# Layer 0 of a four-layer graph network: division as the outputs leave PSUM, first and last norms in halves, and a new order of the matmuls

## The chip, the core and the metric

The kernel runs on one core of a Trainium2 chip, in one launch. The metric is the device time of that launch in microseconds (us). TensorE (PE) multiplies matrices into PSUM (eight banks of 128 x 512 fp32); VectorE (DVE) and ScalarE (ACT) work elementwise; GpSimd (POOL) does little here; SyncE (SP) issues the transfers.

## The reference, cut to what is computed

32 graphs of 512 nodes with 256 features pass through four layers. Each layer is followed by a residual and a norm over the 256 features.

```
x = ln(x + L0(x, adj))   # 4 heads of 64: edges with weights leaky_relu(s_i + d_j), softmax over the edges,
                         # relu(attention @ h + bias) + h, then a norm over each head's 64 columns
x = ln(x + L1(x, adj))   # one head of 256: softmax(relu(s_i + d_j)) over the edges, elu
x = ln(x + L2(x, adj))   # 8 heads of 32, scaled dot products, symmetric edges; norm, feed-forward 256-1024-256, norm
x = ln(x + L3(x, adj))   # one head of 256: softmax(leaky_relu(s_i + d_j)) over the edges
```

The adjacency holds 0 and 1 with ones on the diagonal, so of layer 0's five edge types one occurs. All matmuls but layer 2's scores are in fp32.

## The kernel before

Rows are 128 nodes: a graph is R = 4 rows, its features K = 2 column blocks. `fast_path` does the work; `general_path` is run only when a verdict, kept in `ok` and `sums`, says that the inputs lie outside what the fast path takes.

**The order of the work.** `graph(b)` (L802) is a generator that goes through the stages of graph b: edges, layer 0, layer 1, mask, qkv, attention, projection, feed forward, layer 3. At every `yield`, `paced` (L111) gives out a place, `PERIOD * b` plus an entry of the table `PLACES` (L28), and `heapq.merge` (L832) always continues the graph with the lowest place. With PERIOD 12054, stages of several graphs interleave: layer 0 of one graph runs beside layer 1 of the same, layer 2 of the one before, and layer 3 of another. `tc.manual_schedule` (L831) keeps PE's instructions in exactly that order. The other engines' queues are ordered by a scheduler; each of them works strictly in the order it was given. So the table decides where in PE's stream each group of matmuls stands, and indirectly the rest.

**Layer 0** (L411). For each of four rows, `h0p` gives h and the edge terms; ACT takes exponentials into `ex` and into the last column of `hv` (65 columns a head: 64 values and one weight); DVE adds the bias (L431) and multiplies the values by the weight (L436). Four transposes of a broadcast column (`along`, `gp`, copied by ACT into `gb`) lay out one term per head. Then four blocks j = 0 to 3, one for each row of source nodes. For each block DVE makes four tiles `pt`, one per head (`kept`, L404/L407, 128 x 512). PE then multiplies: for each head two products of 32 value columns with the head's `pt` into `o`, and one product into `den`, whose stationary operand is the head's last 32 columns of `hv`, the weight being the last of them. A product with 32 stationary columns writes 32 rows of PSUM: one of four column groups of the array. The two banks `ops` hold heads 0 and 1, and heads 2 and 3; a head's two halves lie in neighbouring groups:

```
for hh in range(H):
    for e in range(0, HO, DH):
        matmul(ops[hh // 2][hh % 2 * HO + e : hh % 2 * HO + e + DH, :], hv[:, j, hh, e : e + DH], pt[hh])
for hh in range(H):
    matmul(den[hh * DH : (hh + 1) * DH, :], hv[:, j, hh, HC - DH :], pt[hh])
```

So PE's stream in a block is o (head 0, two), o (head 1, two), o (head 2, two), o (head 3, two), den (four). After block 3, ACT copies den and the two o out (`back`, L464), PE transposes each in four pieces (`backp`), DVE takes the reciprocals of den's transposed columns into `rd` (L477), multiplies and applies relu out of PSUM (L484), adds h (L493), and goes on with the norm over heads (`head_layernorm`, L288: sums, differences, squares on ACT, variances, a root by Ln and Exp, a product), gamma (L495), x (L496) and the norm over features (`layernorm`, L268: statistics per row, Ln and Exp for the root, one ACT instruction L280 per row). The next step is layer 1's transposes `xt1p`.

The tiles `pt`, `gb`, `back`, `sq`, `squares`, `relu` and `exp` of stages "a" (layers 0 and 1, edges) share nine buffers (`part`, L257).

**Around layer 0 in PE's stream**, in a middle graph: f2p and f1p of the feed forward, three `o` groups of layer 1 (o<-h,pt, 128 columns), h0p, gp, s (scores), cp, xt3p, block 0, h3p, xt2p, gp, den of layer 2, block 1, qkp, wop (four rows; each row is added by DVE at L680, and the statistics follow), qkp, blocks 2 and 3, four `o` of layer 3 (evacuated by DVE at L752 and L753), ytp, backp, vp, then scores and feed forward.

**The end of a graph.** `feed_forward` (L683) adds the last f2p (L720), then a norm, gamma (L722), x (L723) and another norm for all four rows; layer 3 (L728) divides each row, norms all four, and one transfer of 512 KB writes them (L823).

Of the kernel before, what the change touches and what calls it, by code (L numbers as in the profile page):

```python
# [9 lines left out]
F32 = mybir.dt.float32  # L10
# [18 lines left out]
    "edges": [-3978, -1720, -957, -79],  # L29
    "x": [5375],  # L30
    "mask": [14366, 15324, 18155, 20933],
    "layer 0": [
        -33568, -33515, -33424, -32942, 5301, 7043, 7043, 7043, 8766, 10194, 11091, 11128,
        11993, 11993, 14391,
    ],
    "layer 1": [15460, 15460, 15555, 15555, 15555, 15555, 16382, 17321, 17344, 17344, 17355, 17355],
    "qkv": [18153, 18153, 22255, 22255, 23139, 24065, 25534, 25534, 25534, 25534, 25534],
    "attention": [
        -5960, -4506, -4506, -3927, 26460, 26497, 26497, 26593, 26886, 27435, 27446, 27462,
        28434, 28434, 28779, 29106, 29409, 30200, 31616, 32371, 34290, 34290,  # L40
    ],
    "projection": [34382, 34412, 34412, 34412, 34443],
    "feed forward": [
        36011, 36047, 37566, 38431, 38431, 38519, 38519, 38646, 38646, 38732, 38732, 39499,
        39499, 39646, 39646, 40873, 41200, 41449, 41464,
    ],
    "layer 3": [44919, 44919, 44969, 44969, 44969, 44969, 45682, 48065, 48065, 48065, 48422, 48422],
}
# [24 lines left out]
def fast_path(ctx: ExitStack, tc: tile.TileContext, a: dict, out: bass.AP, bad: bass.AP):  # L73
# [20 lines left out]
    HC = HO + 1  # L94
    ND = R * (H + 2)
    NL = 6
    NV = R * (NL + H) + 2 * K

# [161 lines left out]

    def all_rows(v):
        return v.unsqueeze(1).to_broadcast([P, R, D])

# [3 lines left out]

    def layernorm(y, e, mv):  # L268

        st = buf([P, R, 6], "bn", "bn", 2)  # L270
        rs = buf([P, 2, R], "rs", "rs", 2)
        for r in range(R):
            nc.vector.bn_stats(st[:, r, :], y[:, r, :])  # L273
            nc.vector.bn_aggr(mv[:, r, :], st[:, r, :])  # L274
        inverse_root(rs[:, 0, :], mv[:, :, 1], e)
        nc.vector.scalar_tensor_tensor(  # L276
            rs[:, 1, :], mv[:, :, 0], -1.0, rs[:, 0, :], op0=ALU.mult, op1=ALU.mult
        )
        for r in range(R):
            nc.scalar.activation(  # L280
                y[:, r, :],
                y[:, r, :],
                AF.Identity,
                bias=rs[:, 1, r : r + 1],
                scale=rs[:, 0, r : r + 1],
            )

    def head_layernorm(y, e, var):  # L288

        G = R * H  # L290
        yg = y.rearrange("p r (g d) -> p (r g) d", g=H)
        st = buf([P, 2, G], "lnh", "st", 2)
        nc.vector.tensor_reduce(st[:, 0, :], yg, axis=X, op=ALU.add)
        nc.vector.tensor_scalar_mul(st[:, 0, :], st[:, 0, :], 1.0 / HO)
        nc.vector.tensor_sub(yg, yg, st[:, 0, :].unsqueeze(2).to_broadcast([P, G, HO]))
        for i in range(2):
            g = slice(i * G // 2, (i + 1) * G // 2)
            sq = part("sq").rearrange("p (g d) -> p g d", d=HO)
            nc.scalar.activation(sq, yg[:, g, :], AF.Square, scale=HO**-0.5)
            nc.vector.tensor_reduce(var[:, g], sq, axis=X, op=ALU.add)  # L300
        inverse_root(st[:, 1, :], var, e)
        nc.vector.tensor_mul(yg, yg, st[:, 1, :].unsqueeze(2).to_broadcast([P, G, HO]))

# [106 lines left out]

    def layer0(x, xt, at, rd, mv, var):  # L411
        h = buf([P, R, D], "h", "h0", 2)
# [28 lines left out]
        for j in range(R):  # L441
            pt = [kept("pt0", gbs[hh], at[:, j, :], ex[:, 1, hh, j : j + 1]) for hh in range(H)]
            yield
            for hh in range(H):
                for e in range(0, HO, DH):
                    product(nc.tensor.matmul,
                        ops[hh // 2][hh % 2 * HO + e : hh % 2 * HO + e + DH, :],
                        hv[:, j, hh, e : e + DH],
                        pt[hh],
                        start=j == 0,  # L450
                        stop=j == R - 1,
                    )
            for hh in range(H):
                product(nc.tensor.matmul,
                    den[hh * DH : (hh + 1) * DH, :],
                    hv[:, j, hh, HC - DH :],
                    pt[hh],
                    start=j == 0,
                    stop=j == R - 1,
                )  # L460
        back = []
        for i, o in enumerate((den, *ops)):
            t = part("back")
            nc.scalar.copy(t, o)  # L464
            back.append(t)
        y = sb.tile([P, R, D], F32, tag="y", name="y0", bufs=3)
        for i in range(1 + H // 2):
            yield
            p = bank("backp")
            for r in range(R):  # L470
                product(nc.tensor.transpose,
                    p[:, r * P : (r + 1) * P], back[i][:, r * P : (r + 1) * P], ident
                )
            if i == 0:
                rdh = rd.rearrange("p (i r h) -> p i r h", i=H // 2, r=R)
                for i in range(H // 2):
                    nc.vector.reciprocal(  # L477
                        rdh[:, i],
                        p.rearrange("p (r h e) -> p r h e", r=R, h=H)[
                            :, :, 2 * i : 2 * i + 2, DH - 1  # L480
                        ],
                    )
                continue
            nc.vector.scalar_tensor_tensor(  # L484
                y[:, :, (i - 1) * P : i * P].rearrange("p r (h e) -> p r h e", h=2),
                p.rearrange("p (r h e) -> p r h e", r=R, h=2),
                0.0,
                rdh[:, i - 1].unsqueeze(3).to_broadcast([P, R, 2, HO]),
                op0=ALU.max,
                op1=ALU.mult,  # L490
            )
        nc.vector.tensor_add(x, x, all_rows(bet0))
        nc.vector.tensor_add(y, y, h)  # L493
        head_layernorm(y, 1e-6, var)
        nc.vector.tensor_mul(y, y, all_rows(gam0))  # L495
        nc.vector.tensor_add(y, y, x)  # L496
        layernorm(y, 1e-5, mv[0])
        return y

# [14 lines left out]

    def layer1(x, at, rd, mv):
        xt = yield from transposed([x[:, r, :] for r in range(R)], "xt1")
# [8 lines left out]
        for r in range(0, R, 2):  # L525
# [9 lines left out]
            nc.vector.scalar_tensor_tensor(xr, y, -1.0, xr, op0=ALU.add, op1=ALU.add)  # L535
        layernorm(x, 1e-5, mv[1])
        return x
# [144 lines left out]

    def feed_forward(x, y, mv):  # L683
        layernorm(y, 1e-5, mv[2])
        yt = yield from transposed([y[:, r, :] for r in range(R)], "yt")
# [4 lines left out]
        for r in range(0, R, 2):  # L690
# [29 lines left out]
            nc.vector.tensor_add(yr, acc, yr)  # L720
        layernorm(y, 1e-5, mv[3])
        nc.vector.tensor_mul(y, y, all_rows(ln2g))  # L722
        nc.vector.tensor_add(y, y, x)  # L723
        layernorm(y, 1e-5, mv[4])
        return y


    def layer3(x, at, rd, mv):  # L728
        xt = yield from transposed([x[:, r, :] for r in range(R)], "xt3")
# [20 lines left out]
        for r in range(R):  # L750
# [4 lines left out]
            )  # L755
        layernorm(x, 1e-5, mv[5])
        return x

    ends = [0, R * H, R * (H + 1), ND]
    def load_x(b):  # L760
# [8 lines left out]

    def layer0_all(b, x, xt, at, rd, mv, var):  # L770
        if b == 0:
            bcast(bet0, "bet0")
            bcast(gam0, "gam0")
        return (yield from layer0(x, xt, at, rd, mv, var))

    def layer1_all(b, x, at, rd, mv):
        if b == 0:
            weights13(w1g, "w1g", "a1")
        return (yield from layer1(x, at, rd, mv))

# [11 lines left out]
    def feed_forward_all(b, x, y, mv):  # L792
        if b == 0:
            weights_ff()
        return (yield from feed_forward(x, y, mv))

    def layer3_all(b, x, at, rd, mv):
        if b == 0:
            weights13(w3g, "w3gt", "a3")
        return (yield from layer3(x, at, rd, mv))  # L800

    def graph(b):  # L802
        yield PERIOD * b + PLACES["edges"][0]
        rd = sb.tile([P, ND], F32, tag="rd", name="rd", bufs=3)
        mvs = sb.tile([P, 2 * NL * R + H * R + 2 * K], F32, tag="mvs", name="mvs", bufs=3)
        mv = [mvs[:, 2 * i * R : 2 * (i + 1) * R].rearrange("p (r s) -> p r s", s=2) for i in range(NL)]
        tops = mvs[:, 2 * NL * R :]
        var, spread = tops[:, : H * R], tops[:, H * R :]
        rds = [rd[:, ends[i] : ends[i + 1]] for i in range(3)]
        if b == 0:  # L810
            xt, x = yield from paced(b, "x", load_x(b))
        at = yield from paced(b, "edges", mask(b))
        if b:
            xt, x = yield from paced(b, "x", load_x(b))
        x = yield from paced(b, "layer 0", layer0_all(b, x, xt, at, rds[0], mv, var))
        x = yield from paced(b, "layer 1", layer1_all(b, x, at, rds[1], mv))
        a2 = yield from paced(b, "mask", symmetric(b, at))
# [3 lines left out]
        x = yield from paced(b, "feed forward", feed_forward_all(b, x, y, mv))  # L821
        x = yield from paced(b, "layer 3", layer3_all(b, x, at, rds[2], mv))
        nc.sync.dma_start(out[b].rearrange("(r p) d -> p r d", p=P), x)  # L823
        okd, oks, okv = ok[:, :ND], ok[:, ND : ND + NL * R], ok[:, ND + NL * R :]
# [669 lines left out]
```

## Time and profile before

| | |
|---|---|
| median of 3 runs | 3496.96 us (3496.95 to 3499.22) |
| profiled execution, its own time | 3497.4 us |
| its span, first to last instruction | 3495.6 us, mean granted TensorE clock 0.986 |
| o<-pt,hv (layer 0), 2048 records | 128 x 32 stationary, 128 x 512 moving, 592 ns median of one |
| den<-pt,hv (layer 0), 1024 records | 592 ns |
| backp, 384 records | 273 ns |
| DVE pt, L407, 768 | 743 ns |
| ACT back, L464, from den x32, from o x64 | 585 and 595 ns |
| DVE rd, L477, 64; y, L484, 64; y + h, L493, 32 | 175, 686 and 1225 ns |
| ACT dens, L606 to L608 (layer 2's division), 64 each | 600, 637 and 635 ns, accumulator reads 196 and 199 ns |
| PE waits for graph 0's first norm, before xt1p | 16.4 us |
| PE waits for the last graph's norms, before xt3p | 10.4 us |

Busy times of records that overlap are counted once, while the mean of one record is its whole length: four matmuls that run beside each other show 592 ns each. In a timeline, a row's first number is its start in us from the start of the span, the second the time to the end of the last of its instructions; the bracket tells how long the engine was idle before it and which instruction ended that.

### The profile page before, as it was taken

How to read it: one execution, taken by the hardware profiler on the slowest of the kernel's cores; microseconds unless marked ns; L12 is line 12 of the kernel's file. 1: busy time of each engine (PE TensorE's matmuls, PEld its weight loads, DVE VectorE, ACT ScalarE, POOL GpSimd, SP SyncE). 2: the span in 40 equal slices, each digit the busy share in tenths (PEclk: the TensorE clock that was granted, in tenths of full speed). 3: DMA queues.
4: the chain of work that ended last, by engine and by line, in shares of the span. 5: the costliest groups of instructions: out<-in, count | busy, mean ns of one | idle time of the engine just before them, and what ended most of it. 6: DMA issues, size and time to landing. Idle time of an engine off the chain costs nothing.

```text
span 3495.6 us, 51507 instructions
## 1 busy us (share of the span) xinstructions
PE 3397.5 (97%) x18342; PEld 2366.5 (68%) x18342; DVE 2888.4 (83%) x5178; ACT 2223.0 (64%) x5729; POOL 82.0 (2%) x171
## 2 busy tenths in 40 slices
PE   5799999999999999999999999999999999999986
PEld 3466667776667776667776667776666776666765
DVE  5778888888888888889888889888889888889863
ACT  3556667666667666667666667666667666666652
POOL 0000000000000000000000000000000000000000
PEclk8899999999999999999999999999999999999998
DMA  4334232333232333232333232334332333332220
GB/s 131 85 76 91 61 85 59 81 79 91 62 84 61 79 79 91 64 85 61 76 79 91 67 82 63 74 79 91 69 80 66 71 79 91 71 79 61 45 55 13
DMA packets 164038, 261.01 MB, mean 75 GB/s; under 512 B 20416, under 2 KB 56384, under 8 KB 163776
## 3 DMA queue, kind: packets, MB, share of 16 engines
q1 hardware_dynamic: 163776, 257.65, 32.0%
q8 instruction: 148, 2.42, 0.3%
q14 instruction: 114, 0.93, 0.1%
HBM read 106.57 MB, written 16.78 MB: 35 GB/s over the span
## 4 chain that ended last, share of the span: by engine, by line
PE 94%; DVE 3%; ACT 1%; issue 1%; DMA 1%; SPq 0%; POOL 0%; DVEq 0%; ACTq 0%; POOLq 0%
PE o L104 20%; PE f2p L104 13%; PE f1p L104 13%; PE s L104 8%; PE qkp L104 6%; PE cp L104 6%; PE den L104 5%; PE h3p L104 4%; PE wop L104 3%; PE h1p L104 3%; PE vp L104 3%; PE h0p L104 3%; PE gp L104 2%; PE backp L104 1%; PE xt3p L104 1%
## 5 line engine op out<-in xcount | busy, mean ns | idle before, releaser
L636 DVE TENSOR_TENSOR pr<-pr,a 128x1024 f32<-128x1024 f32 x384 | 454.7, 1217 | 185.4 <-ACT pr L633 185.4
L407 DVE SCALAR_TENSOR_TENSOR pt<-gb,ex,at 128x512 f32<-128x512 f32 x768 | 536.7, 742 | 42.0 <-ACT gb L349 31.6
L633 ACT ACTIVATE pr<-s 128x512 f32<-128x512 f32 x1024 | 545.3, 616 | 3.0 <-PE s L104 3.0
L104 PE MATMUL f2p<-wf,ft 128*128 128x256 f32 x2048 | 484.8, 379 | 5.4 <-ACT ft L706 5.2
L104 PE MATMUL f1p<-yt,wf 128*128 128x256 f32 x2048 | 483.8, 379 | 0.0
L104 PE MATMUL o<-h,pt 128*128 128x257 f32 x2048 | 476.5, 382 | 4.5 <-DVE pt L407 4.4
L104 PEld LDWEIGHTS o<-h,pt 128*128 128x128 f32 x2048 | 386.4, 190 | 99.1 <-issue 44.2
L663 DVE TENSOR_TENSOR pr<-pr 128x1024 f32<-128x1024 f32 x384 | 446.8, 1208 | 2.8 <-PE cp L104 2.8
L104 PEld LDWEIGHTS f2p<-wf,ft 128*128 128x128 f32 x2048 | 383.9, 190 | 63.4 <-ACT ft L706 9.8
L104 PEld LDWEIGHTS f1p<-yt,wf 128*128 128x128 f32 x2048 | 388.5, 190 | 55.0 <-DVE lo L560 0.5
L280 ACT ACTIVATE y<-y,rs 128x256 f32<-128x256 f32 x768 | 398.0, 593 | 17.1 <-DVE rs L276 17.1
L104 PE MATMUL s<-qk 128*128 128x512 f32 x1024 | 377.4, 470 | 4.6 <-DMA qk<-lo 3.8
L706 ACT ACTIVATE ft<-f1p,cols 128x256 f32<-128x256 f32 x512 | 217.0, 469 | 236.6 <-PE f1p L104 235.6
L273 DVE BATCH_NORM_STATS2 bn<-y 128x6 f32<-128x256 f32 x768 | 298.9, 410 | 5.6
L104 PE MATMUL o<-pt,hv 128*32 128x512 f32 x2048 | 286.5, 607 | 8.0 <-DVE pt L407 8.0
L265 ACT ACTIVATE rs<-mvs,eps1e-05_70 128x4 f32<-128x4 f32 x192 | 57.5, 300 | 326.7 <-DVE mvs L274 319.6
L104 PE MATMUL qkp<-xt,wqkv 128*128 128x512 f32 x512 | 240.5, 603 | 0.0
L104 PE MATMUL cp<-pr,v 128*32 128x512 f32 x2048 | 234.2, 595 | 1.4 <-DVE pr L636 1.4
L104 PEld LDWEIGHTS s<-qk 128*128 128x128 f32 x1024 | 189.3, 192 | 55.8 <-issue 27.7
L104 PEld LDWEIGHTS o<-pt,hv 128*32 128x32 f32 x2048 | 73.3, 110 | 179.6 <-issue 94.1
L559 ACT ACTIVATE hi<-qkp,cols 128x512 fp32r<-128x512 f32 x128 | 88.4, 691 | 164.1 <-PE qkp L104 162.1
L752 DVE RECIPROCAL rd<-o 128x1 f32<-128x1 f32 x128 | 21.5, 168 | 177.7 <-PE o L104 177.5
(139 smaller groups left out, 4881.9 us busy)
## 6 DMA issues: line engine op xcount, KB each, us to landing
qk<-hi SPq DMA_DIRECT2D x512, 128.0 KB, 3.4
qk<-lo SPq DMA_DIRECT2D x512, 128.0 KB, 3.5
adjt<-in_adjt SPq DMA_DIRECT2D x64, 512.0 KB, 3.9
adj<-in_adj SPq DMA_DIRECT2D x64, 512.0 KB, 5.0
xt<-in_xt SPq DMA_DIRECT2D x32, 512.0 KB, 3.8
x<-in_x SPq DMA_DIRECT2D x32, 512.0 KB, 5.1
out<-y SPq DMA_DIRECT2D x32, 512.0 KB, 4.5
wf<-in_w1t SPq DMA_DIRECT2D x1, 1024.0 KB, 9.8
```

Of the source, the lines that this page charges most:

```text
L104: latest[0] = what(*args, **kwargs).ins.name
L265: nc.scalar.activation(out, variance, AF.Ln, bias=eps[e])
L273: nc.vector.bn_stats(st[:, r, :], y[:, r, :])
L280: nc.scalar.activation(y[:, r, :], y[:, r, :], AF.Identity, bias=rs[:, 1, r : r + 1], scale=rs[:, 0, r : r + 1],)
L407: nc.vector.scalar_tensor_tensor(t, g, f, edges, op0=ALU.max, op1=ALU.mult)
L559: nc.scalar.activation(hi, p, AF.Identity, bias=bias)
L633: nc.scalar.activation(t[:, i, :], s, AF.Exp, scale=QSCALE)
L636: nc.vector.tensor_mul(t, t, edges)
L663: nc.vector.tensor_add(t, t, u)
L706: nc.scalar.activation(ft[:, f, :], p[:, f, :], AF.Relu, bias=bf1[:, ff + f : ff + f + 1])
L752: nc.vector.reciprocal(rd[:, r : r + 1], p[:, D : D + 1])
```

## The change

- **Order of o, and den on every row.** The two halves of a head's values now go into two banks instead of two column groups: bank e holds columns 32e to 32e + 31 of all four heads, head hh in rows 32hh to 32hh + 31. den's stationary operand is the weight column, broadcast to 32, so that each of its 32 rows holds the head's denominator, in the same rows as o's. The loops around stay as they are.
- **Division.** ACT takes Ln and Exp(-x) of den in PSUM into `inv`; DVE multiplies each bank of o by it on the way out (L474 in the new file). A further ACT Copy of den with an accumulator, and the accumulator of the Exp, feed the verdict in place of the 16 reciprocals per row of nodes. Two groups of transposes instead of three; L489 of the new file applies relu and adds h in one instruction each, so that L493's addition goes.
- **Halves.** For the first and the last graph, `spans(b)` gives two halves of two rows, and layer 0's norms, `layernorm` everywhere, the end of the feed forward and the output transfer run half by half; a half starts when its rows are there. Other graphs have one span of four rows.
- **Places anew**, and four instead of three buffers for `mvs`. PE's stream keeps its contents but for the transposes. In a middle graph gp of layer 0 is in one piece ahead of the last scores, the three o groups of layer 1 stand together, wop is split by a group of qkp (rows 0 and 1, qkp, rows 2 and 3, block 2), and ytp, backp, vp and some scores change places. On DVE, block 0's four pt now stand before the first of six additions L663 (L670 in the new file) instead of after it; the two products L474 stand right behind block 3's last pt.

```diff
@@ -27,24 +27,24 @@
 PERIOD = 12054
 PLACES = {
     "edges": [-3978, -1720, -957, -79],
-    "x": [5375],
-    "mask": [14366, 15324, 18155, 20933],
+    "x": [6086],
+    "mask": [14366, 15398, 19563, 21001],
     "layer 0": [
-        -33568, -33515, -33424, -32942, 5301, 7043, 7043, 7043, 8766, 10194, 11091, 11128,
-        11993, 11993, 14391,
+        -36153, -36100, -36009, -36009, 2373, 3347, 3347, 3351, 8768, 10196, 11113, 11130,
+        13480, 14393,
     ],
-    "layer 1": [15460, 15460, 15555, 15555, 15555, 15555, 16382, 17321, 17344, 17344, 17355, 17355],
-    "qkv": [18153, 18153, 22255, 22255, 23139, 24065, 25534, 25534, 25534, 25534, 25534],
+    "layer 1": [15517, 15517, 15564, 15564, 15564, 15564, 16391, 17330, 17353, 17353, 17353, 17353],
+    "qkv": [15645, 15645, 22398, 22398, 23141, 24048, 25474, 25474, 25557, 25557, 25557],
     "attention": [
-        -5960, -4506, -4506, -3927, 26460, 26497, 26497, 26593, 26886, 27435, 27446, 27462,
-        28434, 28434, 28779, 29106, 29409, 30200, 31616, 32371, 34290, 34290,
+        -5988, -5975, -4578, -3999, 26439, 26452, 26497, 26593, 27411, 27448, 27448, 27464,
+        28436, 28436, 28781, 29108, 29411, 30202, 31600, 31618, 34292, 34292,
     ],
-    "projection": [34382, 34412, 34412, 34412, 34443],
+    "projection": [34462, 34462, 35198, 35198, 35294],
     "feed forward": [
-        36011, 36047, 37566, 38431, 38431, 38519, 38519, 38646, 38646, 38732, 38732, 39499,
-        39499, 39646, 39646, 40873, 41200, 41449, 41464,
+        36011, 36092, 37566, 38486, 38486, 38519, 38519, 38646, 38646, 38732, 38732, 39510,
+        39510, 39648, 39648, 41202, 41202, 41451, 41466,
     ],
-    "layer 3": [44919, 44919, 44969, 44969, 44969, 44969, 45682, 48065, 48065, 48065, 48422, 48422],
+    "layer 3": [44890, 44890, 44940, 44940, 44940, 44940, 46119, 47665, 47665, 47665, 48119, 48119],
 }
 STAGES = {"edges": "a", "x": "a", "layer 0": "a", "layer 1": "a", "feed forward": "c", "layer 3": "c"}
 ALL = mybir.DependencyInfo(mybir.DependencyClass.Sync, mybir.DependencyReason.DATA)
@@ -92,9 +92,9 @@
     NF = F // P
     QSCALE = DH**-0.5
     HC = HO + 1
-    ND = R * (H + 2)
+    ND = R * 2
     NL = 6
-    NV = R * (NL + H) + 2 * K
+    NV = R * (NL + H) + 2 * K + 2
 
     nc.scalar.preload_act_table_set("natural_log_exp_and_others")
     const = ctx.enter_context(tc.tile_pool(name="const", bufs=1))
@@ -258,43 +258,50 @@
 
         return buf([P, N], "part", name, {"a": 9, "c": 5}[stage[0]])
 
-    def all_rows(v):
-        return v.unsqueeze(1).to_broadcast([P, R, D])
+    def all_rows(v, n=R):
+        return v.unsqueeze(1).to_broadcast([P, n, D])
+
+    def spans(b):
+        n = R // 2 if b in (0, B - 1) else R
+        return [slice(r, r + n) for r in range(0, R, n)]
 
     def inverse_root(out, variance, e):
         nc.scalar.activation(out, variance, AF.Ln, bias=eps[e])
         nc.scalar.activation(out, out, AF.Exp, scale=-0.5)
 
-    def layernorm(y, e, mv):
-
-        st = buf([P, R, 6], "bn", "bn", 2)
...
+    def layernorm(y, e, mv, rows):
+
+        for span in rows:
...
@@ -408,7 +415,7 @@
         return t
 
 
-    def layer0(x, xt, at, rd, mv, var):
+    def layer0(b, x, xt, at, spread0, mv, var):
         h = buf([P, R, D], "h", "h0", 2)
         values = hv[:, :, :, :HO]
         ex = buf([P, 2, H, R], "ex", "ex0", 2)
@@ -444,7 +451,7 @@
             for hh in range(H):
                 for e in range(0, HO, DH):
                     product(nc.tensor.matmul,
-                        ops[hh // 2][hh % 2 * HO + e : hh % 2 * HO + e + DH, :],
+                        ops[e // DH][hh * DH : (hh + 1) * DH, :],
                         hv[:, j, hh, e : e + DH],
                         pt[hh],
                         start=j == 0,
@@ -453,48 +460,48 @@
             for hh in range(H):
                 product(nc.tensor.matmul,
                     den[hh * DH : (hh + 1) * DH, :],
-                    hv[:, j, hh, HC - DH :],
+                    hv[:, j, hh, HO:].to_broadcast([P, DH]),
                     pt[hh],
                     start=j == 0,
                     stop=j == R - 1,
                 )
+        inv = part("inv")
+        nc.scalar.activation(inv, den, AF.Ln)
+        nc.scalar.activation(inv, inv, AF.Exp, scale=-1.0, accum_out=spread0[:, 1:2])
         back = []
-        for i, o in enumerate((den, *ops)):
+        for o in ops:
             t = part("back")
-            nc.scalar.copy(t, o)
+            nc.vector.tensor_mul(t, o, inv)
             back.append(t)
+        nc.scalar.activation(inv, den, AF.Copy, accum_out=spread0[:, 0:1])
         y = sb.tile([P, R, D], F32, tag="y", name="y0", bufs=3)
-        for i in range(1 + H // 2):
+
+        def halves(t, i):
+            return t.rearrange("p r (h i e) -> p r h i e", h=H, i=2)[:, :, :, i]
+
+        for i in range(2):
             yield
             p = bank("backp")
             for r in range(R):
                 product(nc.tensor.transpose,
                     p[:, r * P : (r + 1) * P], back[i][:, r * P : (r + 1) * P], ident
                 )
-            if i == 0:
-                rdh = rd.rearrange("p (i r h) -> p i r h", i=H // 2, r=R)
-                for i in range(H // 2):
-                    nc.vector.reciprocal(
-                        rdh[:, i],
-                        p.rearrange("p (r h e) -> p r h e", r=R, h=H)[
-                            :, :, 2 * i : 2 * i + 2, DH - 1
-                        ],
-                    )
-                continue
             nc.vector.scalar_tensor_tensor(
-                y[:, :, (i - 1) * P : i * P].rearrange("p r (h e) -> p r h e", h=2),
-                p.rearrange("p (r h e) -> p r h e", r=R, h=2),
+                halves(y, i),
+                p.rearrange("p (r h e) -> p r h e", r=R, h=H),
                 0.0,
-                rdh[:, i - 1].unsqueeze(3).to_broadcast([P, R, 2, HO]),
+                halves(h, i),
                 op0=ALU.max,
-                op1=ALU.mult,
+                op1=ALU.add,
             )
         nc.vector.tensor_add(x, x, all_rows(bet0))
-        nc.vector.tensor_add(y, y, h)
-        head_layernorm(y, 1e-6, var)
-        nc.vector.tensor_mul(y, y, all_rows(gam0))
-        nc.vector.tensor_add(y, y, x)
-        layernorm(y, 1e-5, mv[0])
+        for span in spans(b):
+            n = span.stop - span.start
+            ys = y[:, span, :]
+            head_layernorm(y, 1e-6, var, span)
+            nc.vector.tensor_mul(ys, ys, all_rows(gam0, n))
+            nc.vector.tensor_add(ys, ys, x[:, span, :])
+            layernorm(y, 1e-5, mv[0], [span])
         return y
 
     def attend(pt, h, r, name):
...
@@ -533,7 +540,7 @@
             nc.vector.scalar_tensor_tensor(y, m, 1.0, y, op0=ALU.min, op1=ALU.add)
             xr = x[:, r : r + 2, :]
             nc.vector.scalar_tensor_tensor(xr, y, -1.0, xr, op0=ALU.add, op1=ALU.add)
-        layernorm(x, 1e-5, mv[1])
+            layernorm(x, 1e-5, mv[1], [span for span in spans(b) if span.stop == r + 2])
         return x
 
 
@@ -718,14 +725,18 @@
                         )
             yr = y[:, r : r + 2, :]
             nc.vector.tensor_add(yr, acc, yr)
-        layernorm(y, 1e-5, mv[3])
-        nc.vector.tensor_mul(y, y, all_rows(ln2g))
-        nc.vector.tensor_add(y, y, x)
-        layernorm(y, 1e-5, mv[4])
+            for span in spans(b):
+                if span.stop != r + 2:
+                    continue
+                ys = y[:, span, :]
+                layernorm(y, 1e-5, mv[3], [span])
+                nc.vector.tensor_mul(ys, ys, all_rows(ln2g, span.stop - span.start))
+                nc.vector.tensor_add(ys, ys, x[:, span, :])
+                layernorm(y, 1e-5, mv[4], [span])
         return y
 
 
-    def layer3(x, at, rd, mv):
+    def layer3(b, x, at, rd, mv):
         xt = yield from transposed([x[:, r, :] for r in range(R)], "xt3")
         h = buf([P, R, D + 2], "h", "h3", 1)
         ex = buf([P, 2, R, 1], "ex", "ex3", 2)
@@ -753,10 +764,13 @@
             nc.vector.scalar_tensor_tensor(
                 x[:, r, :], p[:, :D], rd[:, r : r + 1], x[:, r, :], op0=ALU.mult, op1=ALU.add
             )
-        layernorm(x, 1e-5, mv[5])
-        return x
-
-    ends = [0, R * H, R * (H + 1), ND]
+            for span in spans(b):
+                if span.stop == r + 1:
+                    layernorm(x, 1e-5, mv[5], [span])
+                    rows = out[b].rearrange("(r p) d -> p r d", p=P)
+                    nc.sync.dma_start(rows[:, span, :], x[:, span, :])
+
+    ends = [0, R, ND]
     def load_x(b):
         xt = sb.tile([P, K, N], F32, tag="xt0", name="xt0", bufs=1)
         nc.sync.dma_start(xt, a["xt"][b].rearrange("(k p) n -> p k n", p=P))
```

## The prediction

> **What bounds the kernel now.** I read the page first.
>
> ```profile
> PE 3397.5 (97%) x18342; PEld 2366.5 (68%) x18342; DVE 2888.4 (83%) x5178; ACT 2223.0 (64%) x5729; POOL 82.0 (2%) x171
> ...
> PE 94%; DVE 3%; ACT 1%; issue 1%; DMA 1%; SPq 0%; POOL 0%; DVEq 0%; ACTq 0%; POOLq 0%
> ```
>
> TensorE looks like the only bound. But a matmul's end is modelled, so a busy PE may also be a PE that crawls behind its operands. The cp products of successive graphs start at 340.10, 444.73, 549.36: the period is 104.63 us. Busy time in two parts of one period (us, then PE, PEld, DVE, ACT):
>
> ```profile
> 1517.40:1560.95 43.55, 43.55 (x264) 24.85 (x262) 40.52 (x83) 29.37 (x87) 2.39 (x4) 1.00 0.32 75
> 1560.95:1622.00 61.05, 61.05 (x311) 48.58 (x310) 49.18 (x78) 39.98 (x92) 0.10 (x1) 1.00 0.34 77
> ```
>
> In the first part, which holds all four blocks of layer 0, DVE is 93% busy; in the second it has 12 us to spare. The timeline of DVE in the first part (start, length; in brackets the idle time before and what ended it):
>
> ```profile
> 1517.39 0.69 DVE L720 TENSOR_TENSOR y<-f2p,y 128x512 f32<-128x512 f32 x1 [1.47 <-PE f2p L104]
> ...
> 1519.93 0.16 DVE L276 SCALAR_TENSOR_TENSOR rs<-mvs,rs 128x4 f32<-128x4 f32 x1 [0.63 <-ACT rs L266]
> ...
> 1533.98 2.06 DVE L407 SCALAR_TENSOR_TENSOR pt<-gb,ex,at 128x512 f32<-128x512 f32 x3
> ...
> 1541.64 2.72 DVE L407 SCALAR_TENSOR_TENSOR pt<-gb,ex,at 128x512 f32<-128x512 f32 x4
> ...
> 1557.64 1.41 DVE L407 SCALAR_TENSOR_TENSOR pt<-gb,ex,at 128x512 f32<-128x512 f32 x2
> 1562.99 0.17 DVE L752 RECIPROCAL rd<-o 128x1 f32<-128x1 f32 x1 [3.94 <-PE o L104]
> ```
>
> DVE waits for PE's f2p at 1517.39, then works with about 1 us of idle time until block 3's last pt ends at 1559.05. PE in those blocks:
>
> ```profile
> 1534.41 2.31 PE L104 MATMUL o<-pt,hv 128*32 128x512 f32 x14
> ...
> 1543.82 1.90 PE L104 MATMUL o<-pt,hv 128*32 128x512 f32 x16
> 1545.53 1.04 PE L104 MATMUL den<-pt,hv 128*32 128x512 f32 x8
> 1546.50 0.70 PE L104 MATMUL qkp<-xt,wqkv 128*128 128x512 f32 x1
> ...
> 1558.08 2.08 PE L104 MATMUL o<-pt,hv 128*32 128x512 f32 x16
> 1559.80 1.23 PE L104 MATMUL den<-pt,hv 128*32 128x512 f32 x8
> 1560.95 1.35 PE L104 MATMUL o<-h,pt 128*128 128x257 f32 x5
> ```
>
> A product leaves two records (2048 for 32x4x8 products of o). In block 1, 16 records take 1545.53 - 1543.82 = 1.71 us: four rounds of 0.43 us, four column groups at once. A full block is six rounds, 2.58 us. Block 0 (1534.41 to h3p at 1537.94, 3.53 us) waits for its pts, and block 3's last pt lands one round after the block began. So layer 0's end is set by DVE, the rest of the period by PE.
>
> **The change, part by part, for a middle graph.**
>
> Transposes: three groups of backp become two. Eight took 1567.14 to 1568.01, 0.109 us each; four fewer give -0.44 us, in the PE-bound part.
>
> Division: ACT loses three copies (0.585 + 2 x 0.595 = 1.78 us) and gains Ln, Exp and a summing Copy; L606 to L608 are the same three: 0.600 + 0.637 + 0.635 and two accumulator reads of 0.20, 2.27 us. DVE loses two reciprocals (0.35) and the addition L493 (1.22) and gains two products out of PSUM (L720, same shape, 0.687 each: 1.37). By sums, nothing. But the two products stand in DVE's queue right behind block 3's last pt and wait for den, Ln and Exp; behind them stand lo and the rd of four o3. DVE's 3.94 us of idle there becomes about 5.4, and rd starts some 1.5 us later against PE. The cover is the idle time ahead of DVE's later waits (0.37, 1.67, 3.44 us in that timeline) and eight PSUM banks, of which these hold three until about 3 us after den; without it, 1.5 us a graph. I take 0. den's stationary operand becomes a broadcast; loads of the broadcast ex for gp (137 ns) and of plain back (140 ns) cost the same: 0. The accumulator tiles and the fourth mvs buffer add no instruction: 0.
>
> Order of o: this I take to decide. Before, a head's two products write rows of two column groups, so one pt feeds two groups for two rounds. After, both write the same 32 rows, in two banks, so one pt feeds one group for four. With all four pts there, both fill four groups for four rounds (if the queue looks past waiting records, see below). When the last pt is late, the old block ends 2 + 2 rounds after it, 1.72 us (1559.05 to 1560.95 with 0.18 us of latencies), the new one 4 + 2 rounds, 2.58 us: +0.86 us. DVE's instructions from f2p to block 3's last pt are the same in number and kind; only block 0's pts come earlier, ahead of one L663 (1.18 us), which does not move the end. Price at block 3: +0.86 us; nothing, if the pts were there when the block starts. The same at block 1, where PE arrives at 1543.5 (block 0 ends 0.3 us sooner) and the last pt at 1544.36: it ends at 1546.97, not 1546.40.
>
> Places: wop's rows 2 and 3 now follow a group of qkp (1.81 us). With PE 0.57 us late from block 1, wop's row 2 ends at 1547.07 + 3.54 + 1.82 + 1.81 + 0.91 + 0.17 (latency) = 1555.32; DVE reaches its L680, past two additions and two bn, at about 1554.6: a new wait of 0.7 us, with block 3's four pts queued behind it. Also the last pt of block 3 takes the buffer of block 2's first, free when the first den of block 2 is done: 1556.1 + 2.58 + 0.17 = 1558.9 instead of about 1558.3, 0.6 us late too. Both delay the same pt, so I count 0.65 once; bounds 0 (DVE gets there later) and 0.9 (both rows wait). Earlier gp and later pr<-s may hold cp by up to 0.6 us, but that lies ahead of DVE's end: 0.
>
> Sum for a middle graph: -0.44 + 0.86 + 0.65 = +1.07 us; bounds -0.44 (pts never late; the wait gone too) and +1.3. Over 29 periods: +31 us, bounds -13 and +38.
>
> Edges. The chain of waits at the end has f2p done at 3456.26 and the last xt3p begun at 3468.06. With rows 0 and 1 done under f2p, the second half pays .70 + .75 + .25 of DVE, .70 of ACT and rs, two y (1.1), two half passes (1.3), the second norm and two transposes: about 3.9 us less. At the end two of four y (1.0 us) and half of a 512 KB store go: -1.5. At the start, PE waits 16.4 us for graph 0's first norm: the addition's 1.2 us and about 1 us of row norms are saved, but Ln, Exp, two products and the longer den tail come in: -1, bounds -5 and +2. Edges: -6, bounds -10 and -2.
>
> What is behind four groups at once deserves a rule. The trace has eight products in 1.71 us though each product's two records use the same columns. The Trainium skill, "TensorE: Matmul & The Clock Gate", Part 3, says matmuls stay in strict program order. Strictly in order, each second record would hold back the next group: nine rounds, 3.9 us, before, and 13 rounds, 5.6 us, after, +1.7 us a block or some 218 us in 128 blocks. The measured 1.71 us refutes it for this order, so the sum leaves it out; how far ahead the queue looks, no row shows.
>
> The sum is made against the profiled execution: 3497.4 us, span 3495.6, 0.4 over the median of 3496.96. 3497.4 + 31 - 6 = 3522; against the median 3521.
>
> **Rivals.**
> - *The late pts vanish* (faster). If at block 3 the last pt is there when PE starts it, the only steady term is -0.44 x 32 = -14 and -6 at the edges: 3477. It decides from the point where DVE gains 0.86 us on PE between f2p and that pt. For it: DVE is only 83% busy overall, and the places are set anew. Against: 40.52 busy us in 43.55, and no work taken from this stretch.
> - *Tail only*: +0.86 - 0.44 = 0.42 a graph, 12 us, -6: 3503. For it: DVE need not have reached wop's row 2 yet. Against: four additions are placed as they were, PE is later.
> - *The queue looks not far enough.* A group's four records must be passed before the next group starts; in the old order two. If it cannot, each of three runs of blocks per graph loses one round or two, part of it under the late pts: about +0.86 a graph more, 3521 + 25 = 3546. For it: the old order never needs more. Against: groups do pass each other now.
> - *PSUM or DVE behind the division stalls PE*, 1.5 us a graph: 3565; the idle of DVE speaks against it.
>
> **How the numbers follow.** Forecast 0.50 (own range 3506 to 3532), vanish 0.22, tail only 0.13, queue 0.12, stall 0.03. Within 0.2% is 3490 to 3504, about what a measurement can tell: the tail-only case lies mostly in it. Faster 0.22, same 0.12, slower 0.66. The range 3477 to 3546 leaves out about half of the first rival, and what is beyond the queue's.
>
> **What would show it.** The cp period at 105.5 to 105.8 instead of 104.63; block 3's last pt to the first o3 at 2.7 us, now 1.9; a wait of DVE for wop before block 3; block 1 ending about 2.7 us after its last pt; backp x256; no new PE gap between den and o3; the gap before the last xt3p down from 10.4 to about 7 us. I am wrong if the period falls to 104.2 (pts on time), or if blocks whose pts are all there take longer than 2.6 us (the queue).

## The result, and the profile after

The kernel after takes 3525.83 us (median of 4 runs, 3525.56 to 3527.36), the kernel before 3496.95 (4 runs): ratio 1.0082, 95% interval 1.0065 to 1.0100. It is slower, near the 3521 that were forecast. The profiled execution took 3526.0 us, span 3524.3, clock 0.987 (before 0.986).

Some names that recur: f2p's addition is the DVE instruction at L720 (L727 after) that opens the stretch of the prediction; cp, qkp and wop are products of layer 2; o3 are layer 3's products `o<-h,pt` behind block 3.

The cp products of a middle graph now come every 105.74 us instead of every 104.63. The same two parts of one period as before, in the table by stage (start and end, length, then the busy us and number of instructions of PE, PEld, DVE, ACT and POOL; the last three are the granted clock, the DMA share and GB/s):

```profile
1529.98:1575.07 45.09, 45.09 (x264) 26.14 (x263) 40.67 (x83) 29.28 (x87) 2.39 (x4) 1.00 0.36 78
1575.07:1635.72 60.65, 60.58 (x305) 48.05 (x306) 48.68 (x77) 40.40 (x94) 0.10 (x1) 1.00 0.33 74
```

DVE's work in the first part is what it was (40.67 us, 83 instructions; before 40.52 and 83), yet that part is 1.54 us longer (45.09 against 43.55). The second is 0.40 us shorter (60.65 against 61.05): four transposes fewer. DVE's timeline of the first part (start, length; in brackets idle time and what ended it):

```profile
1529.98 0.69 DVE L727 TENSOR_TENSOR y<-f2p,y 128x512 f32<-128x512 f32 x1 [1.48 <-PE f2p L104]
...
1567.76 0.42 DVE L687 TENSOR_TENSOR y<-wop,y 128x256 f32<-128x256 f32 x1 [0.53 <-PE wop L104]
...
1571.58 0.74 DVE L414 SCALAR_TENSOR_TENSOR pt<-gb,ex,at 128x512 f32<-128x512 f32 x1
1576.56 1.29 DVE L474 TENSOR_TENSOR back<-o,inv 128x512 f32<-128x512 f32 x2 [4.24 <-ACT inv L470]
...
1578.42 0.16 DVE L763 RECIPROCAL rd<-o 128x1 f32<-128x1 f32 x1
```

The wait of 0.53 us for wop is new; in before the four additions stand in one run without it:

```profile
1553.22 1.41 DVE L680 TENSOR_TENSOR y<-wop,y 128x256 f32<-128x256 f32 x4
```

Block 3's last pt ends 42.33 us after the start of L727, 41.66 before. PE's timeline of the same blocks:

```profile
1547.88 1.94 PE L104 MATMUL o<-pt,hv 128*32 128x512 f32 x16
1549.62 1.06 PE L104 MATMUL den<-pt,hv 128*32 128x512 f32 x8
1550.62 3.75 PE L104 MATMUL h3p<-w3g,xt 128*128 128x258 f32 x16
...
1556.49 2.01 PE L104 MATMUL o<-pt,hv 128*32 128x512 f32 x15
...
1559.72 3.70 PE L104 MATMUL qkp<-xt,wqkv 128*128 128x512 f32 x8
...
1571.12 2.30 PE L104 MATMUL o<-pt,hv 128*32 128x512 f32 x13
1572.83 0.62 PE L104 MATMUL den<-pt,hv 128*32 128x512 f32 x2
1572.95 0.90 PE L104 MATMUL o<-pt,hv 128*32 128x512 f32 x2
...
1573.81 1.33 PE L104 MATMUL den<-pt,hv 128*32 128x512 f32 x3
1575.07 2.22 PE L104 MATMUL o<-h,pt 128*128 128x257 f32 x9
```

Block 0 finds its four pts and takes 2.74 us. Blocks 1 and 3 wait for their last pt (it ends at 1556.97 and 1572.32), and what follows them starts 2.75 us later both times: 1559.72 and 1575.07. Before, block 3 had 1.90 us there. A block that finds its pts and has another block behind it takes 2.60 us in both orders (block 2: 1555.48 to 1558.08 before, 1568.52 to 1571.12 after), so the new order costs nothing where the pts are there.

A middle graph in three parts, each a median over 20 graphs, read from the timelines as above; three of the experiments stand beside the two kernels:

| us | f2p's addition to last pt | last pt to first o3 | first o3 to next addition | period |
|---|---|---|---|---|
| before | 41.66 | 1.90 | 61.07 | 104.63 |
| after | 42.33 | 2.75 | 60.66 | 105.74 |
| before, columns of after | 42.36 | 2.75 | 61.07 | 106.17 |
| before, projection's places of after | 41.72 | 1.89 | 61.07 | 104.68 |
| after, wop in one group | 42.08 | 2.75 | 60.66 | 105.49 |

### The profile page after: what moved, and what is told of

The parts are those of the page before. It is cut to its first block, busy times and chain, and to the rows that moved or that the text cites. A ratio compares the mean times of both kernels' runs of the same rounds, so it can differ in the third digit from the quotient of the medians.

```text
span 3524.3 us, 51274 instructions
## 1 busy us (share of the span) xinstructions
PE 3427.3 (97%) x18150; PEld 2394.7 (68%) x18214; DVE 2879.1 (82%) x5174; ACT 2239.4 (64%) x5821; POOL 82.6 (2%) x171
## 3 DMA queue, kind: packets, MB, share of 16 engines
q1 hardware_dynamic: 163808, 257.65, 32.2%
## 4 chain that ended last, share of the span: by engine, by line
PE 94%; DVE 3%; ACT 1%; DMA 0%; issue 0%; SPq 0%; DVEq 0%; ACTq 0%
PE o L104 20%; PE f2p L104 13%; PE f1p L104 12%; PE s L104 8%; PE cp L104 7%; PE qkp L104 6%; PE den L104 5%; PE h3p L104 3%; PE h1p L104 3%; PE wop L104 3%; PE vp L104 3%; PE h0p L104 3%; PE gp L104 2%; PE xt3p L104 1%; PE backp L104 1%; PE ytp L104 1%
## 5 line engine op out<-in xcount | busy, mean ns | idle before, releaser
L670 DVE TENSOR_TENSOR pr<-pr 128x1024 f32<-128x1024 f32 x384 | 447.7, 1210 | 2.6 <-PE cp L104 2.6
L104 PE MATMUL o<-pt,hv 128*32 128x512 f32 x2048 | 315.3, 605 | 6.5 <-DVE pt L414 6.5
L269 ACT ACTIVATE rs<-mvs,eps1e-05_70 128x4 f32<-128x4 f32 (+1 forms) x204 | 60.7, 298 | 387.1 <-DVE mvs L279 379.5
L104 PE MATMUL cp<-pr,v 128*32 128x512 f32 x2048 | 259.3, 596 | 0.3 <-DVE pr L643 0.3
L104 PEld LDWEIGHTS o<-pt,hv 128*32 128x32 f32 x2048 | 100.2, 110 | 149.7 <-issue 135.5
L104 PE MATMUL den<-pt,hv 128*32 128x512 f32 x1024 | 198.8, 595 | 0.0
L104 PEld LDWEIGHTS cp<-pr,v 128*32 128x32 f32 x2048 | 67.3, 109 | 152.0 <-issue 116.6
```

The lines of the kernel that those rows point to most:

```text
L104: latest[0] = what(*args, **kwargs).ins.name
L269: nc.scalar.activation(out, variance, AF.Ln, bias=eps[e])
L670: nc.vector.tensor_add(t, t, u)
```

## The experiments

Twelve kernels ran, five rounds each but for the last (three). Times are medians; the ratio is to the kernel before, run beside them (medians 3495.2 to 3497.4). Times from f2p's addition on are read from one middle graph.

**1. The columns alone**, in the kernel before:

```
-ops[hh // 2][hh % 2 * HO + e : hh % 2 * HO + e + DH, :],
+ops[e // DH][hh * DH : (hh + 1) * DH, :],
...
+y.rearrange("p r (h i e) -> p r h i e", h=H, i=2)[:, :, :, i - 1]   # output view of L484
```

> The kernel before with one part of the change alone: a head's two halves of columns go to one column group of the two o banks (as after), and the division, the places and the norms stay as before. Theory (what sets layer 0's end is the run of rounds that one column group has behind the last pt): 6 rounds of 0.43 us instead of 4, so the last pt of block 3 to the first o3 takes 2.75 us instead of 1.90, the period rises from 104.63 to about 105.5 us, and the time to 3497 + 29 x 0.86 = 3522 us (3515 to 3527). Rival (the order of columns is free, the 1.11 us per graph come from the wop rows and the division): 3497 us, period 104.6. Rival (the new order also changes what passes an unready product): more than 3530 us, with blocks above 2.7 us where all pts are there.

Measured: 3543.27 us, ratio 1.0132 (1.0116 to 1.0147), +1.54 us a graph where 0.86 were expected. The tail behind the last pt grows by 0.85 us, as was counted. The other 0.70 lies ahead of the last pt, and DVE's timeline shows where (its instructions from f2p's addition to the last pt stand in the same order as in before, so the scheduler's order plays no part):

```profile
1576.03 0.42 DVE L677 TENSOR_TENSOR y<-wop,y 128x256 f32<-128x256 f32 x1 [0.28 <-PE wop L104]
...
1580.44 0.75 DVE L407 SCALAR_TENSOR_TENSOR pt<-gb,ex,at 128x512 f32<-128x512 f32 x1 [0.22 <-PE den L104]
```

Block 0 waits for its pts here (the last ends at 1557.49, and h3p follows at 1560.23), so its tail grows by 0.85 us too, and PE's work from there to block 3 is 0.7 to 0.9 us later: wop begins 33.54 us after the addition instead of 32.65, block 2 38.80 instead of 38.09. DVE, which did not wait for wop in a middle graph before, now waits for its fourth row, and the last pt waits for a buffer that block 2's den releases. The column order thus costs twice: once behind the last pt, once through PE's lateness.

**2. The projection's places alone**, in the kernel before:

```
-"projection": [34382, 34412, 34412, 34412, 34443],
+"projection": [34462, 34462, 35198, 35198, 35294],
```

> The kernel before with the places of the projection alone as after: rows 2 and 3 of wop come behind the third group of qkp products. Theory: DVE, which bounds the stretch from f2p to the last pt, now waits about 0.5 us for row 2 of wop, and block 3's last pt comes 0.4 to 0.65 us later: period 105.0 to 105.3, time 3497 + 29 x 0.5 = 3511 us (3506 to 3516). Rival (the column order makes up all of the loss and the DVE wait is taken up by slack): 3497 us, period 104.6.

Measured: 3492.28 us, ratio 0.9989 (0.9980 to 0.9998). The theory missed: +0.05 us a graph. The third addition follows its predecessors without a wait, because two statistics moved in front of it:

```profile
1551.74 0.74 DVE L273 BATCH_NORM_STATS2 bn<-y 128x6 f32<-128x256 f32 x2
1552.40 0.42 DVE L680 TENSOR_TENSOR y<-wop,y 128x256 f32<-128x256 f32 x1
```

The 5 us come from the ends: the second graph's cp starts 3.1 us earlier (231.1 instead of 234.2), and from the last graph's first cp to the end it is 131.4 us instead of 134.9. Why the same places help there, the runs do not show.

**3. The same places taken out of the kernel after**, twice. First with the numbers of before:

> The kernel after with the projection's places as before (four wop rows in a row, ahead of the third group of qkp products). Forecast's theory (the split of the wop rows makes DVE wait, 0.65 us per graph): period 105.1 to 105.4 us, 3507 to 3517 us. Theory after the first four runs (the column order alone makes TensorE 0.85 us later from block 1 on, and with that DVE has to wait for wop rows however they are placed): DVE from f2p to the last pt stays at 42.3 us, period 105.6 to 105.8, 3521 to 3531 us with the edges free by some us.

Measured: 3568.54 us, ratio 1.0210 (1.0196 to 1.0224), period 107.15. This missed what it was to test. A place counts only against its neighbours; after has moved the qkp groups as well, so 34382 lies ahead of all of them, and PE waits for layer 2's division:

```profile
1576.55 3.29 PE L104 MATMUL wop<-wo,ct 128*128 128x256 f32 x14 [1.57 <-DVE ct L618]
```

So the four rows were put behind the second group, with `"projection": [34462, 34462, 34462, 34462, 35294]`:

> The kernel after with all four wop rows at 34462, which puts them in a row behind the second and ahead of the third group of qkp products, the order that before has. Theory (column order alone makes TensorE late from block 1 on, DVE then waits for wop rows in either order): DVE from f2p to the last pt stays 42.2 to 42.4 us, period 105.6 to 105.8, 3520 to 3530 us. Forecast's term (the split costs 0.65 us per graph): period 105.1, 3507 us.

Measured: 3516.66 us, ratio 1.0065 (1.0051 to 1.0079), period 105.49. Neither number: the split costs 0.25 us a graph in after. What stays, 42.08 against 41.66 us, is there without the split; the buffer now holds the last pt:

```profile
1569.93 0.75 DVE L414 SCALAR_TENSOR_TENSOR pt<-gb,ex,at 128x512 f32<-128x512 f32 x1 [0.22 <-PE den L104]
```

**4. The loops exchanged**, so that products next to each other go to four groups:

```
-for hh in range(H):
-    for e in range(0, HO, DH):
+for e in range(0, HO, DH):
+    for hh in range(H):
```

> The kernel after with the two loops around layer 0's products exchanged, so that products next to each other go to four different column groups; the same products on the same groups in all. Theory: no change beyond 0.15% (3521 to 3531 us), because the last pt still has 6 rounds of its own column group behind it; the last pt to o3 stays 2.75 us. It may even cost a little, as products of the late head now stand ahead of the second halves of the others. Rival (TensorE's queue is held by two products on one group in a row, and a mixed order lets four groups run): 2 rounds less per graph, 3526 - 29 x 0.86 = 3501 us.

Measured: 3524.78 us, ratio 1.0081 (1.0068 to 1.0095), period 105.76. PE's timeline of block 3:

```profile
1571.32 2.73 PE L104 MATMUL o<-pt,hv 128*32 128x512 f32 x15
...
1575.27 2.00 PE L104 MATMUL o<-h,pt 128*128 128x257 f32 x8
```

The last pt to o3 stays 2.75 us. How products stand in the queue is not the cause; how much of one group hangs on the last pt is.

**5. The halves alone**, in the kernel before (the norms and the output of the first and last graph as after):

> The kernel before with the halves of rows in the first and last graph and the output in halves, and nothing else of the change. Theory: only the edges move: the tail gives back 3 to 4 us (gap before the last xt3p 7.3 us instead of 10.4), the head between -1 and +1: 3493 us (3491 to 3496), period 104.63 in the middle as before. Forecast's own term for the edges: -6, which would be 3491. Rival (places that were made for whole norms let the halves collide with other work): 3497 us or more.

Measured: 3491.55 us, ratio 0.9986 (0.9977 to 0.9995), period 104.64. The gap before the last xt3p is the same in both kernels (first fence this one, second after):

```profile
3461.20 1.82 PE L104 MATMUL xt3p<-ident,y 128*128 128x128 f32 x6 [7.30 <-ACT y L285]
```

```profile
3496.41 1.82 PE L104 MATMUL xt3p<-ident,y 128*128 128x128 f32 x6 [7.30 <-ACT y L285]
```

From the last graph's first cp to the end it is 130.45 us here, 131.49 after, 134.90 before. At the start, the third graph's cp comes 2.5 us earlier than before (337.48 against 340.02), in after 0.4 later (340.39). In graph 0, after starts backp 3.3 us later than this kernel (42.09 against 38.79): its blocks end 0.9 us later (the columns alone make backp 0.8 us later, 39.30 instead of 38.46 in before), and PE waits 3.06 us for the divided o, against 0.69 here.

**6. The wait filled.** If the tail behind the last pt is the loss, other work of PE must be able to fill it. Row 0 of o3 is moved from behind block 3 to ahead of it, in both kernels (its entry among layer 3's places):

```
-"layer 3": [44890, 44890, 44940, 44940, 44940, 44940, 46119, 47665, ...
+"layer 3": [44890, 44890, 44940, 44940, 44940, 44940, 46119, 47280, ...
```

> The kernel after with one place moved: the first row of layer 3's products (o3) goes ahead of block 3 of layer 0 instead of behind it. Theory (what the change loses is TensorE's wait for the last pt and the 6 rounds of one column group behind it): o3's first row (1.74 us) now fills the wait, block 3 finds all its pts and takes 2.6 us, so the second row of o3 comes 1.33 us earlier (45.5 us after f2p instead of 46.83): period about 104.4, time 3526 - 29 x 1.33 = 3487 us (3480 to 3496), below the kernel before. Rival (the loss is DVE's or the division's, which still come after block 3, now 0.4 us later): period 105.7 to 106.1, 3526 to 3538 us.

> The same move in the kernel before. Theory: there the last pt has only 4 rounds behind it and block 3 takes 2.87 us, against 2.6 with all pts there: a gain of 0.25 us per graph, period 104.4, 3497 - 7 = 3490 us (3486 to 3494). So the two kernels come to within 0.2 us per graph of each other. Rival (the move is worth the same in both, about 1.3 us): 3459 us. Rival (no gain): 3497.

Measured: after 3502.80 us, ratio 1.0014 (1.0005 to 1.0023), period 104.84, -0.90 where -1.33 was expected; before 3501.17, ratio 1.0013 (1.0004 to 1.0022), 104.77, +0.14 where -0.25 was expected. Both miss by 0.4 us, and their difference falls from 1.11 to 0.07 us, as expected. The move of the kernel after:

```profile
1559.46 1.95 PE L104 MATMUL o<-pt,hv 128*32 128x512 f32 x16
1561.20 1.06 PE L104 MATMUL den<-pt,hv 128*32 128x512 f32 x8
1562.20 2.00 PE L104 MATMUL o<-h,pt 128*128 128x257 f32 x8
1564.13 1.94 PE L104 MATMUL o<-pt,hv 128*32 128x512 f32 x16
1565.87 1.06 PE L104 MATMUL den<-pt,hv 128*32 128x512 f32 x8
1566.86 3.74 PE L104 MATMUL o<-h,pt 128*128 128x257 f32 x16
```

Start to start, a block followed by o3 takes 2.73 or 2.74 us; followed by another block, in after, 2.60 (1568.52 to 1571.12). The o3 row between blocks takes 1.93, two in a row 3.58. So a change between products on column groups and full ones costs about 0.14 us, and this order has two more. The next kernel moves the row ahead of block 2 (47260), with no more changes than after has:

> The kernel after with the first row of o3 ahead of block 2, so that blocks 2 and 3 stand next to each other. Theory: the 0.4 us by which the move ahead of block 3 missed its number are changes between products on column groups and full ones (0.14 to 0.17 us each, two more of them there); here there are as many as in after, so the second row of o3 comes 1.2 to 1.3 us earlier than in after: period 104.45 to 104.55, 3488 to 3492 us. Rival (the 0.4 us are DVE's or the division's): period 104.85 again, 3503 us.

Measured: 3491.18 us, ratio 0.9988 (0.9979 to 0.9997), period 104.52; the 0.4 us are almost all back.

```profile
1555.97 1.90 PE L104 MATMUL o<-h,pt 128*128 128x257 f32 x8
1557.80 1.94 PE L104 MATMUL o<-pt,hv 128*32 128x512 f32 x16
...
1560.40 1.94 PE L104 MATMUL o<-pt,hv 128*32 128x512 f32 x16
...
1563.12 3.74 PE L104 MATMUL o<-h,pt 128*128 128x257 f32 x16
```

Blocks 2 and 3 take 2.60 and 2.72 us; neither waits.

**7. The wait ahead of block 1 filled as well**, with the first qkp group (`"qkv": [15645, 15645, 22249, 22398, ...`), on top of the first move of 6:

> The kernel after with the first row of o3 ahead of block 3, and the first of the qkp groups ahead of block 1, where TensorE also waits (3.23 us for a block that takes 2.6 with all pts there). Theory: another 0.4 to 0.6 us per graph, as TensorE is no longer late for the wop rows: period about 103.9, 3470 to 3478 us. Rival (DVE bounds the stretch, and the two lo it now makes ahead of the pts delay block 2's and 3's): no more than after_o3_first has, 3487 us or more.

Measured: 3532.57 us, ratio 1.0101 (1.0085 to 1.0116), period 105.71. The stretch from f2p's addition to the row of o3 behind block 3 gains only 0.17 us (45.92 to 45.75), and 0.95 us are lost in another place: at layer 1's transposes and the f2p behind them.

```profile
1520.46 1.26 PE L104 MATMUL xt1p<-ident,y 128*128 128x128 f32 x8
1522.28 2.00 PE L104 MATMUL f2p<-wf,ft 128*128 128x256 f32 x8 [0.56 <-ACT ft L713]
```

From xt1p to f2p it takes 1.82 us instead of the 0.87 of the first kernel of 6. The norm ahead of xt1p comes later on ACT (its four instructions end 8.96 us after cp's start instead of 6.99), and ft, which f2p waits for, stands behind it there.

**8. The best of both**, the kernel before with the halves and row 0 of o3 ahead of block 2:

> The kernel before with the halves of the first and last graph and the first row of o3 ahead of block 2. Theory: 0.1 to 0.2 us per graph less than before_halves, period 104.45 to 104.55, 3491.5 - 5 = 3486 us (3484 to 3490), the lowest so far. Rival (the move costs here as it did ahead of block 3, +0.15 per graph): 3496 us.

Measured: 3484.61 us, ratio 0.9969 (0.9957 to 0.9981), period 104.45. It is faster than both kernels.

**9. Less work for DVE**, the kernel before without L722 (its output lacks that factor):

> The kernel before without layer 2's multiplication by the last norm's gain (ln2g), one DVE operation of 1.2 us per graph inside the stretch from f2p to the last pt; the output lacks that factor. Theory (DVE sets the length of that stretch in before): the last pt of block 0 and of block 3 come up to 1.1 us earlier, until TensorE's own work is the bound: 0.7 to 1.1 us per graph, period 103.5 to 103.9, 3465 to 3477 us. Rival (TensorE or ScalarE's chain through cp sets it): period 104.6, 3497 us.

Measured: 3576.39 us, ratio 1.0231 (1.0216 to 1.0247), period by turns 106.75 and 108.4. It tells nothing of the theory: the scheduler, given less DVE work, put layer 2's last four norms on ACT ahead of the exponentials that the third row's gp needs.

```profile
1559.38 2.10 ACT L280 ACTIVATE y<-y,rs 128x256 f32<-128x256 f32 x4
...
1561.60 0.32 PE L104 MATMUL gp<-ident,ex 128*128 128x128 f32 x1 [1.75 <-ACT ex L427]
```

That DVE alone sets the length of the stretch in before was therefore not shown by taking work away.

## Why the prediction was right, point by point

A middle graph was forecast at +1.07 us and measured at +1.11. Its terms, with what the runs gave each:

| term, us a graph | forecast | measured | from |
|---|---|---|---|
| four transposes fewer | -0.44 | -0.41 | 61.07 to 60.66, old against new division |
| two rounds more behind block 3's last pt | +0.86 | +0.85 | 1.90 to 2.75, experiment 1 |
| last pt itself later | +0.65 | +0.67 | 41.66 to 42.33 |
| division (Ln, Exp, two products of DVE) | 0 | about 0 | 2.75 behind the last pt with the old one too; behind the first o3 -0.41, where the transposes' -0.44 were counted |

*Order of o.* Right in size and place: six rounds of one column group behind a late pt instead of four. Experiment 4 takes away the order in the queue as a cause, 6 shows that the price is gone when PE need not wait for the pt. Under "Places" the prediction put the "new wait of 0.7 us" down to the rows of wop behind a group of qkp, on top of PE's 0.57 us from block 1 (measured 0.62: qkp begins 29.73 us after the addition instead of 29.11); beside it stood the buffer that block 2 frees 0.6 us late, and it counted the two once. The size held, 0.67 for 0.65, but the first of the two causes weighs less than it was given: the split alone costs 0.05 us in before and 0.25 in after, and 0.42 of the 0.67 stay without it, with the buffer holding the last pt. Experiment 1 shows that the column order alone makes such a delay, by PE's lateness behind a block that ends late; it reaches the last pt as a wait for wop or for the buffer, whichever the order leaves. That in after it is block 1 rather than block 0 is read from the timeline only. With the split, the wait for wop hides the one for the buffer, so counting them once was right.

*Division.* Its two products do stand behind block 3's last pt: DVE's idle there is 4.24 us (about 5.4 were foreseen) and rd starts at 1578.42, 3.35 us after the first o3 (before 1562.99 - 1560.95 = 2.04, so 1.3 us later, near the 1.5 foreseen). No gap of PE to speak of follows from it in a middle graph (0.07 us idle in the 60.65 of the second part). The rival that PSUM or DVE stalls PE for 1.5 us a graph is out. The division was not run without the new columns: its factor lies in the rows that the new order gives to o.

*cp held.* The forecast allowed up to 0.6 us; it is 0.9 (4.53 us for the 32 records instead of 3.64), because the last two pr<-s stand behind four norms on ACT (they begin at 1544.55 and 1545.23, while cp began at 1542.40). It lies ahead of DVE's end, and block 0 then finds its pts. So block 0 ends 0.09 us later than before and not 0.3 sooner; this came to nothing, since block 1's end hangs on its last pt.

*Edges.* Forecast -6, measured -3.6: 28.6 us in all by the profiled executions, 32.2 in 29 periods. The halves are worth what was thought (-5.8 alone); the start was mis-sized, +0.4 instead of -1, and the end -3.4 instead of -5.4. The new places of the projection alone also gained some 6 us at the ends (experiment 2), so -3.6 is a sum of gains and losses that these runs do not take apart. Of the 3.6 us by which the difference of the profiled executions (28.6) exceeds the forecast one (25), 2.4 lie here and 1.2 in the middle graphs.

*Rivals.* The late pts did not vanish, and tail only (+0.42 a graph) is refuted by the last pt's 0.67. The queue does look far enough: blocks that find all their pts take 2.60 us, followed by a full product 2.74. In the block that waits, products of den run ahead of those of o that stand before them (two records of den begin at 1572.83, ahead of two of o at 1572.95); this is the same thing that the prediction read from the eight products in 1.71 us, and again not the strict program order that the Trainium skill states ("TensorE: Matmul & The Clock Gate", Part 3).

## What to carry to other kernels

Where the last operand of a group of column-tiled products comes late, count the rounds that its own column group still has to do: spread one operand's products over groups, or put other work of TensorE ahead of the group so that it finds all operands there. A block that ends late costs a second time when another engine waits for TensorE's next results, so follow the delay to the next wait. And test a place or an order by the neighbours it gets, not by its number.

## What the hardware showed that was not expected

Going from products on 32 columns to full ones, or back, costs about 0.14 us each time: 2.74 us for a block of 24 records ahead of full products, 2.60 ahead of another block; 1.93 us for a row of o3 between two blocks, 1.79 in a run. Two changes more a graph went with 0.3 us (periods 104.84 and 104.52). What causes it, no run shows.
